# Layer 0's expert stage: the base product cut into 2x2 blocks with seven block products, and two table builds moved behind the first gathers

## The chip, the cores and the metric

The kernel runs on one core of one Trainium2 chip, in one launch. The metric is the device time of that core in microseconds. Most executions of one kernel agree within 0.3%.

## The reference

The input x has 8 sequences of 128 tokens with 512 features, so 1024 tokens. Four layers follow each other, each with a conditioning block whose output goes into an expert block, and the expert block's output is added to x. All data are 32-bit floats. What matters here is the expert block of layer 0 and what stands around it:

```
y    = L0_cond(x)                        # gated feed-forward with low-rank terms, 1376 wide
base = einsum('bsd,od->bso', y, base_W)  # 512 -> 512, the product that is changed
mid  = einsum('bsd,edr->bser', y, lora_A) * top2_weights(softmax(y @ router_W.T))
x    = x + base + einsum('bser,erd->bsd', mid, lora_B) * 2
x    = x + L1_ffn(L1_cond(x))            # low ranks only: needs all of the new x
x    = x + L2_ffn(L2_cond(x, caches))    # attention over a paged cache and the new tokens
x    = x + L3_ffn(L3_cond(x))
```

The attention of layer 2 rotates queries and keys by tables of sines and cosines, and hides cache positions beyond each sequence's length by a mask.

## The kernel before

Activations lie transposed: features on the 128 partitions in four chunks, tokens along the row. `x` is a tile of [128, 4, 1024], and so is `y0`, the output of layer 0's conditioning block. Engine names as in the profile: PE is the matrix engine, DVE the vector engine, ACT the scalar engine, POOL the general engine, which also issues the gathers, and SP issues most transfers.

Many products here are already made in 2x2 blocks with seven block products in place of eight (the Strassen-Winograd scheme): the gate and up products (`gates_by_seven`), the down product (class `Down`), the query, key and value projections and the output projection (`seven`). There each operand is cut into four blocks a11..a22 and b11..b22, four sums s1..s4 of the weight blocks and four differences t1..t4 of the token blocks are made by DVE or POOL, and the seven products are a11b11, s2t2, s1t1, s3t3, a12b21, s4b22 and a22t4. PE accumulates in PSUM; DVE reads half-finished sums out (`u`, `p1`) while PE goes on adding onto the same place.

Layer 0's expert block is made by the helper `experts`, for two halves of 512 tokens, g = 0 and 1. `mids(g)` makes expert ranks and router logits, `route(g)` the top-2 weights on DVE, `mix(g)` turns the weighted ranks so that they can be multiplied again, and `outs(g, os)` makes the output rows: for each of four 128-row chunks `o` a PSUM bank of 512 tokens takes four plain base matmuls and one with `wB` (the experts' second factor). `add_to_x` then adds the bank to `x` on DVE (L305). The order of calls is written out by hand:

```
        mix0(0, large_bank)
        outs0(0, (0, 1), large_bank)
        mids0(1, small_bank)
        route0(1)
        outs0(0, (2, 3), large_bank)
        mix0(1, small_bank)
        outs0(1, (0, 1), large_bank)
        adapted = adapt(0)
        outs0(1, (2, 3), large_bank)
        mids1(0, small_bank)
        route1(0)
        att.begin()
        att.begun(adapted)
```

`adapt(g)` (tile `t1_g`, masked into `l1`) and `mids1`, `route1`, `mix1`, `outs1` are layer 1, which needs the final x of its half. `att.begin` starts the first loads and gathers of attention: the weights, `gather(0, "k")` and `gather(0, "v")` (16 indirect transfers on POOL), and the sums of the projection's weights (`W[0].factors()`, tile `q_s`, L886, on DVE). `att.begun` turns the gathered keys (`kt`, L1119), writes them out and fetches them (`kT`), and issues the next gather, whose buffers are free when `kt` is made.

Ahead of all that, where `attention` is entered, DVE makes the key positions and the mask (`kpos` L820, `hide` L822 and L828) and POOL makes the rotation tables `tsk`, `txk`, `tsq`, `txq` (eight instructions, L838). Their memory is free when layer 0's down product has ended.

A scheduler may move instructions of an engine against each other within what the data allow; those that pass through `kept` or `held` (`tc.keep_in_program_order`) stay in the order of the text.

Of the kernel before, what the change touches and what calls it, by code (L numbers as in the profile page):

```python
# [10 lines left out]
F32 = mybir.dt.float32  # L11
I32 = mybir.dt.int32
AF = mybir.ActivationFunctionType
ALU = mybir.AluOpType
# [3 lines left out]
P = 128  # L18
NB = 8
NT = NB * P  # L20
# [5 lines left out]
HQ, HK, HD = 32, 8, 128  # L26
# [6 lines left out]
NEG = -1e30  # L33
# [14 lines left out]
def forward(ctx: ExitStack, tc: tile.TileContext, a: dict, out: bass.AP):  # L48
    nc = tc.nc
    pe, act, dve, pool, sp = nc.tensor, nc.scalar, nc.vector, nc.gpsimd, nc.sync  # L50
# [13 lines left out]
    wop = ctx.enter_context(tc.tile_pool(name="wop", bufs=1))  # L64
    rp = c1.enter_context(tc.tile_pool(name="rp", bufs=1, side="right"))

    x = xpool.tile([P, DC, NT], F32, tag="x", name="x")
# [4 lines left out]
    st = cg.enter_context(tc.tile_pool(name="st", bufs=2))  # L72
# [34 lines left out]
    for k in range(7):  # L107
        n = 1 << k
# [17 lines left out]
    part = of_partition("part", p_div32, 32.0, ALU.mult, p_mod32)  # L126
# [44 lines left out]
    lens = ints("seqlens", NB)  # L171
# [145 lines left out]
    wmr0 = load_small(ew, "wmr0", [P, DC, 136], chunks(a["wmr0"]), tag="wmr")  # L317
# [5 lines left out]
    with c0:  # L323
# [310 lines left out]
        def psp_bank(shape, name):  # L634
            return psp.tile(shape, F32, tag="mm", name=name)

        HB_ = []
        downs = [Down(0, k) for k in range(2)]

# [20 lines left out]
        downs = [Down(1, k) for k in range(2)]  # L660
        downs[0].begin()
        downs[0].go_on()
        mids0, route0, mix0, outs0 = experts("l0", wmr0, "probs", 2.0, None, wB0, base0, y0, add_to_x)[:4]
        mids0(0, psp_bank)
        route0(0)
        downs[1].begin()
# [9 lines left out]
    with psa:  # L676
# [9 lines left out]


        att = attention(tc, a, x, ident, lens, kvrow, part, ww, wop, ypool, sums, rot, eps, ps_, c2, chunks, mm)

        l1 = att.scratch([P, DC * P + NT], "l1")  # L690
        wa1 = l1[:, 0 : DC * P].rearrange("p (c r) -> p c r", c=DC)
        sp.dma_start(wa1, chunks(a["wa1"]))
# [11 lines left out]
            mid_of=lambda tok: [(t1[:, tok], w11)],  # L704
        )[:4]

        mix0(0, large_bank)
        outs0(0, (0, 1), large_bank)
        mids0(1, small_bank)
        route0(1)  # L710
        outs0(0, (2, 3), large_bank)
        mix0(1, small_bank)
        outs0(1, (0, 1), large_bank)
        adapted = adapt(0)
        outs0(1, (2, 3), large_bank)
        mids1(0, small_bank)
        route1(0)
        att.begin()
# [82 lines left out]
def attention(tc, a, x, ident, lens, kvrow, part, ww, wop, ypool, sums, rot, eps, psa, c2, chunks, mm):  # L801
# [14 lines left out]


    kpos = ap.tile([P, 4], F32, tag="kpos", name="kpos")
    for c in range(4):
        dve.tensor_scalar(kpos[:, c : c + 1], part, float(c * P), None, ALU.add)  # L820
    hide = ap.tile([P, NB, 4], F32, tag="hide", name="hide")
    dve.tensor_tensor(  # L822
        hide,
        kpos.unsqueeze(1).to_broadcast([P, NB, 4]),
        lens.unsqueeze(2).to_broadcast([P, NB, 4]),
        ALU.is_ge,
    )
    dve.tensor_scalar(hide, hide, NEG, None, ALU.mult)  # L828


    tabs = {}
    for m in ("k", "q"):
        ws = ap.tile([P, NB, HD], F32, tag="ts" + m, name="ts" + m)
        wx = ap.tile([P, NB, HD], F32, tag="tx" + m, name="tx" + m)
        for dst, w, tr in ((ws, straight[m], "cos"), (wx, crossed[m], "sin")):
            for i in range(2):
                h = slice(i * 64, (i + 1) * 64)
                pool.tensor_tensor(  # L838
                    dst[:, :, h], w[:, h].unsqueeze(1).to_broadcast([P, NB, 64]), trig[tr], ALU.mult
                )  # L840
        tabs[m] = (ws, wx)


    half = ap.tile([P, 2, REP + 1], F32, tag="half", name="half")
# [23 lines left out]
    def kept(i):  # L868
        return tc.keep_in_program_order(i) if running or i.ins.engine == pool.engine else i
# [38 lines left out]
    def every(ops):  # L908
        for _ in ops:
            pass  # L910

    def gather(n, what):
        qd, p = steps[n]
        t = []
        for j in range(2):
            if what == "k":
                d = kvp.tile([P, 4, HD], F32, tag="kn", name=f"kn_{n}_{j}")
            else:
                d = vals[n % 2 * 2 + j]
            for c in range(4):  # L920
                i = (2 * p + j) * 4 + c
                kept(pool.indirect_dma_start(  # L922
                    out=d[:, c, :], out_offset=None, in_=kc if what == "k" else vc,
                    in_offset=bass.IndirectOffsetOnAxis(ap=kvrow[what][:, qd, i : i + 1], axis=0),
                ))
            t.append(d)
        S[n][what + "c"] = t
# [186 lines left out]
    def turn_cached(n):  # L1114

        s = S[n]
        t = wk.tile([P, 4, 8, 32], F32, tag="kt", name=f"kt_{n}", bufs=1)
        for j in range(2):
            kept(dve.transpose(  # L1119
                t[:, :, 4 * j : 4 * j + 4, :], s["kc"][j].rearrange("p c (b d) -> p b c d", b=4)  # L1120
            ))
        s["kT"] = wk.tile([P, 4, 8, 32], F32, tag="kT", name=f"kT_{n}")
        written(turned[n], t)
        return lambda: kept(sp.dma_start(s["kT"], turned[n].rearrange("b i a m d -> (b i) a m d")))
# [150 lines left out]

    Y = []

    def scratch(shape, name):
        return wk.tile(shape, F32, tag="pT", name=name)

    late = []

    def begin():
        weights(0)
        out_weights(0)
        gather(0, "k")
        gather(0, "v")
        every(W[0].factors())

    def begun(behind):  # L1290

        with tc.issue_after(behind.ins):
            turn_cached(0)()
        gather(1, "k")

    def first(mixed, outs_):
# [1037 lines left out]
```

## Time and profile before

| | |
|---|---|
| three runs | 1492.9, 1496.06, 1497.18 us (median 1496.06) |
| profiled execution | 1490.35 us, its span 1488.6 us |
| granted PE clock | 0.999 |
| PE busy | 1476.6 us, 99% of the span |
| DVE busy | 1065.6 us, 72% |
| POOL busy | 856.4 us, 58% |
| ACT busy | 562.0 us, 38% |
| 243 to 296 us of the span | PE 52.46 us busy of 53, DVE 25.92, POOL 34.53, ACT 4.66 |

Times inside the span count from its first instruction. The stage that is changed lies between 243 and 296 us. In the trace each 32-bit matmul of the program shows as two records, so a row with x8 is four matmuls. A row gives the start, the time until the end of its last record (ends of matmuls are modelled and overlap the next start), the engine, the line, the tiles and the number of records; idle time just ahead of it, and what ended it, stand in square brackets.

### The profile page before, as it was taken

What the parts mean: (1) busy time and instruction counts of PE and PEld (TensorE: products, weight loads), DVE (VectorE), ACT (ScalarE), POOL (GpSimd) and SP (SyncE); (2) the same over time, 40 slices, a digit from 0 to 9 for tenths busy, and PEclk for the clock granted to TensorE, in tenths of its full rate; (3) what the DMA queues carried; (4) which work ended last, traced back from release to release, by engine and by line L of the source; (5) the groups of instructions that cost most, each with busy time, mean ns of one, the idle gap of its engine ahead of it and who ended that gap; (6) DMA issues with size and microseconds to landing.
All of it is one profiled execution on the core that took longest, in us unless ns stands there. A gap on an engine that the chain in (4) does not pass through costs nothing.

```text
span 1488.6 us, 18093 instructions
## 1 busy us (share of the span) xinstructions
PE 1476.6 (99%) x5603; PEld 938.3 (63%) x5603; DVE 1065.6 (72%) x2121; ACT 562.0 (38%) x1422; POOL 856.4 (58%) x876
## 2 busy tenths in 40 slices
PE   9999999999999999999999999999999999999998
PEld 7888787455555655555555555565555555558887
DVE  4665425388888787787778778787878878855475
ACT  1111101044545544454554454454445455431110
POOL 2241104567777777776777777677777777622310
PEclk9999999999999999999999999999999999999999
DMA  7411001213545444564454455345445534433001
GB/s 242 118 44 32 1 1 55 94 36 115 183 148 173 150 119 129 150 183 126 135 152 131 128 158 177 110 135 163 129 125 166 168 106 138 120 104 98 1 9 52
DMA packets 155257, 171.44 MB, mean 115 GB/s; under 512 B 52624, under 2 KB 125776, under 8 KB 155024
## 3 DMA queue, kind: packets, MB, share of 16 engines
q1 hardware_dynamic: 136976, 133.18, 30.0%
q0 software_dynamic: 17056, 36.49, 7.7%
q8 instruction: 47, 0.77, 0.2%
q10 hardware_dynamic: 1120, 0.52, 0.1%
q14 instruction: 58, 0.48, 0.1%
HBM read 129.36 MB, written 40.76 MB: 114 GB/s over the span
## 4 chain that ended last, share of the span: by engine, by line
PE 96%; DVE 2%; ACT 0%; DMA 0%; issue 0%; DVEq 0%; ACTq 0%; SPq 0%
PE st L1173 18%; PE av L1225 18%; PE g L367 9%; PE q_six L979 8%; PE wo_two L979 6%; PE q_one L979 6%; PE q_five L979 6%; PE dn L367 5%; PE wo_six L979 4%; PE wo_one L979 4%; PE eo_l L53 3%; PE z L1761 2%; PE h L1761 2%; PE midp_l L53 1%; PE o L1761 1%; PE gu L367 1%
## 5 line engine op out<-in xcount | busy, mean ns | idle before, releaser
L922 POOL DMA_INDIRECT kn<-in_k_cache,kvrow_k x256 | 272.2, 1063 | 77.1 <-issue 71.2
L922 POOL DMA_INDIRECT vals<-in_v_cache,kvrow_v x256 | 272.3, 1064 | 73.6 <-issue 60.2
L1225 PE MATMUL av<-pT,vals 128*128 128x512 f32 x640 | 290.8, 592 | 0.2 <-DVE oT L1235 0.2
L1177 ACT ACTIVATE pT<-st,hide 128x512 f32<-128x512 f32 x256 | 175.9, 687 | 192.0 <-PE st L1173 178.8
L1173 PE MATMUL st<-qT,kT 128*128 128x512 f32 x512 | 237.4, 596 | 0.0
L1225 PEld LDWEIGHTS av<-pT,vals 128*128 128x128 f32 x640 | 121.4, 190 | 152.7 <-issue 148.3
L1078 POOL TENSOR_TENSOR vq<-q,txq 128x256 f32<-128x256 f32 x128 | 121.1, 976 | 130.6 <-ACT sqq L1052 92.9
L1173 PEld LDWEIGHTS st<-qT,kT 128*128 128x128 f32 x512 | 97.2, 191 | 109.3 <-issue 103.3
L1193 DVE TENSOR_TENSOR part<-pT 128x512 f32<-128x512 f32 x128 | 88.3, 691 | 76.2 <-ACT pT L1177 62.8
L979 PE MATMUL q_one<-q,x 128*128 128x384 f32 x256 | 93.0, 486 | 0.0
L1052 ACT ACTIVATE sqq<-q 128x128 f32<-128x128 f32 x252 | 78.2, 310 | 10.4 <-DVE q L1028 3.8
L979 PEld LDWEIGHTS q_one<-q,x 128*128 128x128 f32 x256 | 48.5, 190 | 39.8 <-issue 14.3
L979 PE MATMUL q_six<-q_s,xs_all 128*128 128x384 f32 x192 | 69.8, 486 | 0.0
L1033 ACT COPY q<-q_one 128x256 f32<-128x256 f32 x32 | 11.9, 372 | 151.9 <-PE q_one L979 133.5
L979 PE MATMUL wo_one<-o,oT 128*128 128x256 f32 x256 | 65.9, 380 | 1.1 <-ACT k L1033 0.8
L1173 PE MATMUL st<-qT,kTn 128*128 128x512 f32 x128 | 65.4, 592 | 0.0
L979 PE MATMUL wo_two<-o_s,os 128*128 128x256 f32 x256 | 60.6, 379 | 0.3 <-DVE os L938 0.3
L1177 ACT ACTIVATE pT<-st,rs 128x512 f32<-128x512 f32 x64 | 44.0, 687 | 38.5 <-PE av L1225 18.5
L979 PEld LDWEIGHTS wo_one<-o,oT 128*128 128x128 f32 x256 | 48.5, 190 | 15.0 <-issue 1.9
L436 POOL TENSOR_TENSOR ws<-wu 128x256 f32<-128x256 f32 (+1 forms) x9 | 6.4, 711 | 86.8 <-DMA wu<-in_WuT 79.8
L1209 ACT COPY rows<-rows 32x32 f32<-32x32 f32 x96 | 20.7, 216 | 92.1 <-DVE rows L1204 91.4
L367 PE MATMUL g<-xs,ws 128*128 128x256 f32 (+1 forms) x240 | 55.1, 379 | 0.0
(461 smaller groups left out, 2838.5 us busy)
## 6 DMA issues: line engine op xcount, KB each, us to landing
turned_new<-qkt SPq DMA_DIRECT2D x120, 160.0 KB
turned_cached<-kt SPq DMA_DIRECT2D x128, 128.0 KB
kT<-turned_cached SPq DMA_DIRECT2D x32, 512.0 KB
R<-sums SPq DMA_DIRECT2D x32, 512.0 KB
qT<-turned_new SPq DMA_DIRECT2D x30, 512.0 KB
q<-in_WqT SPq DMA_DIRECT2D x8, 1024.0 KB
o<-in_WoT SPq DMA_DIRECT2D x8, 1024.0 KB
kn<-in_k_cache,kvrow_k POOLq DMA_INDIRECT x256
```

The costliest lines, as they stand in the source:

```text
L53: pe.matmul(o, lhsT, rhs, start=start, stop=stop)
L367: pe.matmul(o, lhsT, rhs, start=start, stop=stop, skip_group_check=True)
L922: kept(pool.indirect_dma_start(out=d[:, c, :], out_offset=None, in_=kc if what == "k" else vc, in_offset=bass.IndirectOffsetOnAxis(ap=kvro ...
L979: kept(pe.matmul(o, l[:, c, :], r[:, c, :], start=start and c == 0, stop=c == 1, skip_group_check=True))
L1052: kept(act.activation(sq, S[n][m][:, j, i, :], AF.Square, accum_out=S[n]["ssq"][:, j, col : col + 1]))
L1078: kept(pool.tensor_tensor(to, t[:, b, :, hi : hi + 64], wx[:, b, lo : lo + 64].unsqueeze(2).to_broadcast(list(to.shape)), ALU.mult,))
L1173: kept(pe.matmul(ps, s["kT"][:, c, 4 * j : 4 * j + 4, :] if c < 4 else s["kn"][:, j], s["qT"][:, :, REP * j : REP * (j + 1), :].rearrange( ...
L1177: kept(act.activation(pT[:, c, :, :].rearrange("p i t -> p (i t)"), ps, AF.Exp, **(dict(bias=hide[:, b, c : c + 1]) if c < 4 else dict(bia ...
L1193: kept(dve.tensor_tensor(o, l, r, ALU.add))
L1209: kept(act.copy(rows[0:32, g, :], rows[32 * g : 32 * g + 32, 0, :]))
L1225: kept(pe.matmul(ps, v[:, c, :], pT[:, c, :, :].rearrange("p i t -> p (i t)"), start=c == 0, stop=c == NC - 1, skip_group_check=True,))
L1761: return pe.matmul(o, lhsT, rhs, start=start, stop=stop, skip_group_check=True)
```

## The change

Layer 0's base product is made in 2x2 blocks too. `experts` is called without `base` for layer 0, so that its `outs` is no longer used there. `base_sums` makes s1..s4 of the base weights (eight DVE instructions of 256 elements) before `mids0(0)`. `block_sums(g, t)` makes t1..t4 of y0 for a half (four DVE instructions of 512 elements). The class `Based(g, k)` stands for two output chunks of one half: two PSUM banks, `even` and `odd`, each with two halves of 256 tokens. `begin` multiplies a11b11 and copies it to `p1` on ACT. `go_on` makes the other six products, with three DVE reads of half-finished sums between. `finish` adds the `wB` products, lets DVE add `u` or `p1` to x three times from SBUF, and then adds the four PSUM halves to x.

`kpos` and `hide` move into `hidden()`, called from `att.begun`; the rotation tables move into `tabled()`, called at the end of `att.begin`, behind the first 16 gathers; `W[0].factors()` moves from `att.begin` to the end of the block in `att.begun`.

```
+        A0 = base_sums()
-        mids0, route0, mix0, outs0 = experts("l0", ..., wB0, base0, y0, add_to_x)[:4]
+        mids0, route0, mix0, _, _, T0 = experts("l0", ..., wB0, None, y0, None)
...
+            def into(self, o, l, r, start=False):
+                for c in range(2):
+                    pe.matmul(o, l[:, c, :], r[:, c, :], start=start and c == 0, stop=False, skip_group_check=True)
+
+            def begin(self):
+                self.into(self.even[:, 0], A0[self.k][0], self.b[0][0], True)
+                held(act.copy(self.p1, self.even[:, 0]))
+                return self
+
+            def go_on(self):
...
+                self.into(odd[:, 1], s1, t1, True)
+                self.into(odd[:, 0], s2, t2)
+                held(dve.tensor_tensor(u, odd[:, 0], p1, ALU.add))
+                held(dve.tensor_tensor(p1, odd[:, 1], p1, ALU.add))
+                self.into(even[:, 1], s3, t3)
+                held(dve.tensor_tensor(p1, even[:, 1], p1, ALU.add))
+                self.into(odd[:, 1], s4, b22)
+                self.into(even[:, 0], a12, b21)
+                self.into(even[:, 1], a22, t4)
+
+            def finish(self):
...
+                    pe.matmul(ps, wB0[...], T0[g][...], start=False, stop=True, skip_group_check=True)
+                for t, _, more in at.values():
+                    if more is not None:
+                        held(dve.tensor_tensor(t, t, more, ALU.add))
+                for t, ps, _ in at.values():
+                    held(dve.tensor_tensor(t, ps, t, ALU.add))
...
+        based = [Based(0, k).begin() for k in range(2)]
+        block_sums(0, [yt0[:, n] for n in range(4)])
         mix0(0, large_bank)
-        outs0(0, (0, 1), large_bank)
         mids0(1, small_bank)
+        for b in based:
+            b.go_on()
+            b.finish()
         route0(1)
-        outs0(0, (2, 3), large_bank)
+        block_sums(1, [t[:, n] for t in yt1 for n in range(2)])
+        based = [Based(1, k).begin() for k in range(2)]
         mix0(1, small_bank)
-        outs0(1, (0, 1), large_bank)
+        based[0].go_on()
+        based[0].finish()
         adapted = adapt(0)
-        outs0(1, (2, 3), large_bank)
+        based[1].go_on()
+        based[1].finish()
         mids1(0, small_bank)
...
     def begin():
         weights(0)
         out_weights(0)
         gather(0, "k")
         gather(0, "v")
-        every(W[0].factors())
+        tabled()

     def begun(behind):
         with tc.issue_after(behind.ins):
             turn_cached(0)()
+            hidden()
+            every(W[0].factors())
         gather(1, "k")
```

As built, PE has nineteen rows more, the scheduler puts a product of the next block into some of the gaps (two of block (0,1) ahead of s4b22 of block (0,0)), POOL's eight table instructions stand behind the first 16 gathers and ahead of the next eight, and SP's load of the first output weights (`o`), which waits for the last base matmul, stands ahead of the last of the four writes of `kt`. From the turn of layer 1's first half (`mix1(0)`) on, every engine's order is the same as before.

## The prediction

> **What bounds the kernel now.** The page's busy times and its chain that ended last come first.
>
> ```profile
> PE 1476.6 (99%) x5603; PEld 938.3 (63%) x5603; DVE 1065.6 (72%) x2121; ACT 562.0 (38%) x1422; POOL 856.4 (58%) x876
> PE 96%; DVE 2%; ACT 0%; DMA 0%; issue 0%; DVEq 0%; ACTq 0%; SPq 0%
> ```
>
> PE is the bound: idle 12.0 us of 1488.6, and 96% of the chain. So work taken from PE counts in full, work put on DVE, ACT or POOL counts only where PE then waits for it, and time won elsewhere counts for nothing. Next the stage itself, in the timelines of PE and of DVE and POOL.
>
> ```profile
> 212.14 2.32 PE L367 MATMUL dn<-h,wds 128*128 128x256 f32 x10
> 214.30 2.32 PE L367 MATMUL dn<-h,wd 128*128 128x256 f32 x10
> ...
> 255.80 3.60 PE L53 MATMUL eo_l<-y,base 128*128 128x512 f32 x8
> 259.23 1.02 PE L53 MATMUL eo_l<-midT_l,wB 128*128 128x512 f32 x2
> 260.09 3.60 PE L53 MATMUL eo_l<-y,base 128*128 128x512 f32 x8
> ...
> 291.19 0.73 PE L53 MATMUL midp_l<-w,l 128*128 128x136 f32 x4 [0.47 <-DVE l L309]
> ```
> ```profile
> 210.25 0.42 DVE L609 TENSOR_TENSOR du_dn<-dn,dp_dn 128x256 f32<-128x256 f32 x1 [5.23 <-PE dn L367]
> 210.71 0.42 DVE L610 TENSOR_TENSOR dp_dn<-dn,dp_dn 128x256 f32<-128x256 f32 x1
> ...
> 244.91 0.95 DVE L822 TENSOR_TENSOR hide<-kpos,seqlens 128x32 f32<-128x32 f32 x1
> 245.89 1.17 DVE L828 TENSOR_SCALAR hide<-hide 128x32 f32<-128x32 f32 x1
> 251.42 3.25 DVE L886 TENSOR_TENSOR q_s<-q 128x768 f32<-128x768 f32 x2 [2.73 <-DMA q<-in_WvT]
> 254.60 1.94 DVE L886 TENSOR_TENSOR q_s<-q,q_s 128x768 f32<-128x768 f32 x2
> ```
> ```profile
> 250.65 3.21 POOL L838 TENSOR_TENSOR txq<-wx_q,sin 128x512 f32<-128x512 f32 x2
> 279.09 0.94 POOL L922 DMA_INDIRECT kn<-in_k_cache,kvrow_k  x1 [4.10 <-DVE kt L1119]
> ```
>
> PE's groups stand start to start without a gap: eight records of 512 columns take 259.23 - 255.80 = 3.43 us (0.429 each), ten of 256 take 2.16 us (0.216 each). Half the columns cost half the time; the smaller matmul pays 1 ns. The only wait of PE that the timeline shows between 243 and 296 us is 0.47 us. DVE is busy 25.92 of these 53 us.
>
> **PE's work.** Removed are eight groups of base products (four chunks, two halves), 8 x 3.43 = 27.4 us. Added are four blocks of seven products of two matmuls, 4 x 7 x 2 x 2 = 112 records of 256 columns, 112 x 0.2158 = 24.2 us. The `wB` products go from 16 records of 512 (6.87 us) to 32 of 256 (6.91 us). On PE: **-3.25 us**. All of it is on the path.
>
> **Sums of the base weights.** Eight DVE instructions of 0.42 us, 3.4 us. Their tile takes over the place of the down product's weight sums, whose last reader for chunk pair 0 ends near 214.3 us. DVE then has nothing until the logits at 224.67 (idle 11.90 us there). They lie under PE's `dn` groups: nothing; without that cover, 3.4 us.
>
> **Differences of y0.** Half 0: four DVE instructions of 512 elements, 0.69 us each, behind the last copy of y0 at 244.55, so until 247.3. Meanwhile PE has two a11b11 (1.73 us), the turn of the ranks (0.43) and `midp` (3.7), from 243.0 to 248.9: nothing. Half 1's four stand 5 us and more ahead of their use: nothing.
>
> **The hand-overs.** In each block PE must wait, before s4b22, until DVE has read both halves of `odd`, and before a22t4 until it has read s3t3. I lay PE's built order against DVE's, with 0.34 us start to start for independent 256-element instructions and 0.46 where one needs the one before (both in the rows of `y<-dn` and `du_dn`, `dp_dn`). Block (0,0): PE has s3t3 and one product of block (0,1) in between, 1.73 us; DVE needs 0.04 to see the end, two reads and one instruction of `route0(1)` between them, about 1.9: PE waits 0.2. Block (0,1): cover 2.2 us, but two differences of half 1 (0.6 to 0.69 each) stand between the reads: 0.1. Block (1,0): cover s3t3 and a quarter of `adapt(0)`, 1.73 us against 0.9: nothing. Block (1,1): cover 1.3 us; the mask of `l` and two `kt` (1.9 us) stand ahead of the reads, and they are just in time: nothing, with 0.1 us to spare. Sum **+0.3 us**.
>
> **The tail of the stage.** `q_s` moves from 251 us, where DVE had time, to about 280 to 286, four instructions of 0.95. They stand among the last block's adds and ahead of layer 1's first `route`. That chain ends in `mw_l`, which PE needs for its next turn of ranks. It ends about 288 us in the new time, while PE's last `t` ends 0.6 us earlier. PE's small waits here were about 0.8 us in all (0.47 shown, the rest under 0.2 each) and become 1.1: **+0.3 us**. From the other side: the same line has taken 943 to 2017 ns. At 2.0 us four of them bring 4.3 us more, of which PE would wait for all; at the low end nothing. I take 0.95, since the long ones stand beside POOL's arithmetic and POOL issues gathers here.
>
> **The moved tables and mask.** The 16 gathers begin 10.7 us earlier (POOL's tables took 243.31 to 253.80); nobody waited for them, as `kt` at 278.12 follows `t` of PE: gain nothing. The eight table instructions now run from about 263 to 274 us, ahead of `gather(1, "k")`, which waits for `kt` (about 278) anyway; they are used at 304 us: nothing. The mask is used at 320 us: nothing. On SP the load of `o` now holds one write of `kt` back until the last base matmul, about 282 us; the fetch of `kT` goes out at about 286, as now (285.35), and its use is at 316 us: nothing.
>
> What can cost is the neighbourhood of tables and DVE. In the rows above `hide` takes 0.95 and 1.17 us for 32 elements while the tables run, where such a size takes 0.19 elsewhere (`e_l`), and two `q_s` take 3.25 us against 1.94 for the next two; the adds from PSUM in the same stretch (`y<-dn`, 0.42) are not slower. [...] I take 0; the upper end, if a read stands behind a delayed add, is 2 us.
>
> **Sum.** -3.25 + 0.3 + 0.3 = -2.65 us, 0.18% of the profiled execution (1490.35; span 1488.6). Behind the stage PE has no gap before the end and keeps the gain. The three runs had a median of 1496.06, 5.7 above the profiled one; on that median I predict **1493.4 us**. Differences within 0.3% (4.5 us) are about what a measurement of this kernel can tell from no change, so the likeliest true effect is a gain that lies inside that band.
>
> **Rivals.** (1) The saving is given back: the hand-overs and the tail cost as much as PE gains, with `q_s` at its median 1.46 us (4 x 0.5 = 2 us) and 1 us more of waits: 1496.1. For it: the cover is one or two products of 0.86 us, where the down product, made in the same way without a PE wait, had 2.16 us for each. Against: the order laid out above leaves only tenths. (2) Slower: DVE becomes the bound of the stage. DVE's work rises by the blocks' 4 x 10 x 0.42 = 16.8 us, the differences' 5.5, less eight adds of 0.69, from 25.9 to 42.7 us in about 50. If DVE runs late at every hand-over by one blocked instruction (1.23 us, the table's), eight hand-overs cost 9.8 us: -3.25 + 9.8 gives +6.6, 1502.6. It decides from 0.97 us of mean delay on, (4.5 + 3.25) / 8. Against: only two hand-overs lie within the table's 11 us, and DVE still has 7 us of idle time. (3) The change does not save PE time, because twice as many, smaller matmuls pay a fixed price: the 0.429 and 0.216 us speak against it; at 10 ns a record the 64 records more cost 0.6 us, so this cannot turn the sign.
>
> More than -3.25 - 0.8 = -4.1 us can't come, since PE's waits in the stage are no more than 0.8 us.
>
> **How the numbers follow.** The forecast has 0.73, rival 1 0.16, rival 2 0.11, rival 3 is inside the forecast. Under the forecast the true effect lies inside the band, but the three runs lie from 3.2 below to 1.1 above their median, and the edge (1491.6) is only 1.8 us below my number: I give 0.31 to a measured gain over 0.3%, 0.41 to the band and 0.01 to a loss. Rival 1 gives 0.03, 0.11 and 0.02; rival 2 0.01 to the band and 0.10 to a loss. Together 0.34 faster, 0.53 the same, 0.13 slower. The range goes from 1489.0 (the largest gain, 1492.0, less 3 us of spread) to 1499.0 (rival 1 with 3 us more for the long `q_s`); rival 2 is left out.
>
> **What would show it.** PE busy falls by 3.2 us; rows of `b_..` at 0.216 us a record; in the stretch from the end of `dn` to the first `q_one` PE idle about 1.4 us, in brackets behind DVE; base sums between 214 and 222 us; tables near 263 to 274 with DVE's adds slowed beside them; the first `st` 2.7 us earlier than 318.90. Wrong would be: waits of 1 us or more at s4b22 or a22t4 (rival 2), `q_s` of 1.5 us or more with a PE wait behind `mw_l` (rival 1), records of 256 columns above 0.22 us (rival 3), or a difference that arises behind 320 us, where I expect none.

## The result, and the profile after

The changed kernel takes 1512.80 us (median of 6 runs, 1508.42 to 1516.68) against 1494.52 us for the kernel before: ratio 1.0115, 95% interval 1.0099 to 1.0130. It is slower by 1.15%, and the medians lie 18.3 us apart, where a gain of 2.65 us was forecast. The profiled execution took 1514.16 us with a span of 1512.4 us, 23.8 more than the profiled execution before (1488.6).

First the page of the changed kernel: busy times, and the chain that ended last.

```profile
PE 1480.8 (98%) x5667; PEld 954.0 (63%) x5667; DVE 1087.0 (72%) x2169; ACT 563.5 (37%) x1426; POOL 855.4 (57%) x876
PE 91%; DVE 4%; DMA 2%; issue 1%; another core or an unknown queue 1%; SPq 0%; ACT 0%; POOL 0%; DVEq 0%; ACTq 0%
```

PE's busy time has not fallen by 3.2 us but risen by 4.2, though it does less arithmetic, and its share of the chain went from 96 to 91%, DVE's from 2 to 4. Where that happens shows in the timeline of PE (start, time, records, and in brackets the idle time before and what ended it).

```profile
249.78 3.62 PE L728 MATMUL b<-yt,base0s 128*128 128x256 f32 x16
258.93 2.08 PE L728 MATMUL b<-y,base0s 128*128 128x256 f32 x4 [5.53 <-DVE b0u L742]
263.93 2.07 PE L728 MATMUL b<-y,base 128*128 128x256 f32 x4 [2.93 <-issue]
...
280.68 2.08 PE L728 MATMUL b<-y,base0s 128*128 128x256 f32 x4 [7.49 <-DVE b0u L743]
```

Three waits of 15.95 us in all: before s4b22 and a22t4 of block (0,0), and before s4b22 of block (0,1). They cost more than their length: sixteen records ahead take 3.6 us, 0.22 each, but four records behind a wait take 1.86 us start to start (263.93 to 265.79), 0.47 each. The windows (PE, PEld, DVE, ACT, POOL busy, then the granted clock) show why.

```profile
258.00:263.00 5.00, 2.08 (x4) 1.18 (x4) 1.20 (x4) 0.00 (x0) 3.78 (x5) 0.58 0.16 53
263.00:268.00 5.00, 4.07 (x10) 3.27 (x11) 4.55 (x4) 0.00 (x0) 4.68 (x5) 0.50 0.12 37
...
278.00:283.00 5.00, 2.32 (x6) 1.87 (x7) 4.66 (x13) 0.00 (x0) 0.00 (x0) 0.50 0.02 5
```

The granted clock is 0.58, 0.50 and 0.50 in these three windows (1.00 in 253 to 258 us), so PE is "busy" for longer with the same work. Now the other side of the hand-over, DVE and ACT, and POOL beside them.

```profile
253.99 0.42 DVE L266 TENSOR_TENSOR r_l<-r_l,lower 128x256 f32<-128x256 f32 x1
257.78 0.42 DVE L742 TENSOR_TENSOR b0u<-b,b0u 128x256 f32<-128x256 f32 x1 [3.37 <-remote]
...
263.45 0.42 DVE L745 TENSOR_TENSOR b0u<-b,b0u 128x256 f32<-128x256 f32 x1 [4.25 <-remote]
...
263.91 11.33 DVE L765 TENSOR_TENSOR x<-x,b0u 128x256 f32<-128x256 f32 x3
```
```profile
252.06 0.39 ACT L241 COPY mid_l<-midp_l 128x272 f32<-128x272 f32 x1 [3.31 <-PE b L728]
```
```profile
263.83 0.96 POOL L1020 DMA_INDIRECT vals<-in_v_cache,kvrow_v  x1 [0.30 <-issue]
264.80 2.50 POOL L937 TENSOR_TENSOR tsk<-ws_k,cos 128x512 f32<-128x512 f32 x2
...
272.15 2.47 POOL L937 TENSOR_TENSOR txq<-wx_q,sin 128x512 f32<-128x512 f32 x2
```

Two different things went wrong. The addition at L742 waits for nothing but PE's s2t2, which is the second quarter of the sixteen records at 249.78 and over by about 251.5; yet DVE begins at 257.78, 6 us later, and the profile finds no releaser ("remote"). ACT's copy of `midp`, whose records end at about 249.9, begins 2.1 us late in the same way. And the three additions at L765, which take 1.1 us together when alone, take 11.33 us here. One of them alone is held for 10.7 us: nearly the whole stretch of the eight table instructions (264.80 to 274.62).

From the start of the last `dn` record to the start of the first `q_one`, "the stage" from here on, the profile before has 242.71 to 295.65, 52.9 us; the profile after has 243.50 to 316.17, 72.7 us. Of the 23.8 us more, 19.7 arise here, 0.8 before and 3.3 behind.

### The profile page after: what moved, and what is told of

The parts are those of the page before. It is cut to its first block, busy times and chain, and to the rows that moved or that the text cites. A ratio compares the mean times of both kernels' runs of the same rounds, so it can differ in the third digit from the quotient of the medians.

```text
span 1512.4 us, 18286 instructions
## 1 busy us (share of the span) xinstructions
PE 1480.8 (98%) x5667; PEld 954.0 (63%) x5667; DVE 1087.0 (72%) x2169; ACT 563.5 (37%) x1426; POOL 855.4 (57%) x876
## 4 chain that ended last, share of the span: by engine, by line
PE 91%; DVE 4%; DMA 2%; issue 1%; another core or an unknown queue 1%; SPq 0%; ACT 0%; POOL 0%; DVEq 0%; ACTq 0%
PE st L1271 17%; PE av L1323 17%; PE g L367 9%; PE q_six L1077 8%; PE q_one L1077 5%; PE q_five L1077 5%; PE wo_two L1077 5%; PE dn L367 5%; PE wo_one L1077 3%; PE wo_six L1077 3%; PE h L1861 2%; PE z L1861 2%; PE o L1861 1%; PE midp_l L53 1%; PE b L728 1%
## 5 line engine op out<-in xcount | busy, mean ns | idle before, releaser
L1020 POOL DMA_INDIRECT vals<-in_v_cache,kvrow_v x256 | 272.4, 1064 | 73.6 <-issue 59.3
```

Source lines behind the costliest of these rows:

```text
L1020: kept(pool.indirect_dma_start(out=d[:, c, :], out_offset=None, in_=kc if what == "k" else vc, in_offset=bass.IndirectOffsetOnAxis(ap=kvro ...
```

## The experiments

Kernels that were sent together (a set) ran on the same chip beside the kernel before. In some of these sets what waited for PE began at once (within 0.1 us of the record's end, on time below), in others 2 to 9 us late in parts of the stage (late below) in every kernel whose gathers run beside the blocks; so times are compared within a set, and each run below says which of the two its set was. The kernel before took 1489.09 and 1489.38 us in the sets on time and 1491.21 to 1494.52 us in the late ones and in the result. Theory 1 is that the tables hold DVE instructions beside them (one addition for 10.7 us in the profile after), a cost that the prediction had put at nothing; the rivals are the early gathers (theory 2, later 4) and hand-overs that are too tight in themselves (theory 3).

### First set: blocks alone, moves alone, two other places for the tables

**e1**, everything moved is put back:

```diff
+    hidden()
+    tabled()
...
     def begin():
-        tabled()
+        every(W[0].factors())
     def begun(behind):
-            hidden()
-            every(W[0].factors())
```

> The blocks as changed, but mask, rotation tables and the sums q_s where they stood before (tables ahead of the first gathers). Theory 1 (lock): adds of two SBUF tiles on DVE are held while POOL's tables stand back to back beside the blocks. Theory 2 (early gathers): gathers that begin 10 us earlier delay DVE's reads (waits of 3.4 and 4.3 us with no releaser). Theory 3 (blocks): the hand-overs themselves are too tight. Before is about 1494.5. By 1 and 2 no long add and no waits at the hand-overs, 1491 to 1493; by 3 waits of several us at s4b22 stay, 1500 or more.

Measured: 1494.64 us, ratio 1.0034 (1.0022 to 1.0046), stage 57.6 us, on time. DVE, then POOL, then PE:

```profile
246.24 1.82 DVE L772 TENSOR_TENSOR yt<-y 128x512 f32<-128x512 f32 x1
248.09 1.65 DVE L772 TENSOR_TENSOR yt<-y,yt 128x512 f32<-128x512 f32 x1
```
```profile
245.01 2.50 POOL L937 TENSOR_TENSOR txk<-wx_k,sin 128x512 f32<-128x512 f32 x2
247.46 3.41 POOL L937 TENSOR_TENSOR tsq<-ws_q,cos 128x512 f32<-128x512 f32 x2
```
```profile
257.71 2.08 PE L728 MATMUL b<-y,base0s 128*128 128x256 f32 x4 [3.32 <-DVE b0u L743]
```

Beside the tables a difference of y0 takes 1.65 to 1.82 us for 0.69, and two table instructions take 3.41 for 2.5. From 246.24 to 253.01 us DVE makes four differences, 1.57 to 1.85 us start to start, and POOL's last four table instructions take 6.75 us: in these rows the two engines take turns, one instruction each. The first hand-over is 3.3 us late, and the four records behind it take 2.08 us, where four take 1.13 in e3. The blocks alone, with the old places, lose 5.6 us against the kernel before (1489.09).

**e2**, the plain base product with the moves; the edit is against the kernel before:

```diff
... (the bodies of mask and tables become hidden() and tabled())
         gather(0, "k")
         gather(0, "v")
-        every(W[0].factors())
+        tabled()
...
             turn_cached(0)()
+            hidden()
+            every(W[0].factors())
         gather(1, "k")
```

> The plain base product as before, but mask, tables and q_s moved as in the change. Theory 1: nothing of two SBUF tiles that PE waits for lies beside the tables, so within 1 us of before (1493.5 to 1496). Theory 2: the ACT copy and DVE steps of the second half's route come 2 to 8 us late, but PE has base matmuls in front of it: 0 to +4 us. Theory 3: the same as before.

Measured: 1489.59 us, ratio 1.0004 (0.9992 to 1.0016), stage 52.8 us, on time. The moves alone cost nothing that these runs can tell.

**e3**, the tables by memsets in the same place:

```diff
-                    kept(pool.tensor_tensor(dst[:, :, h], ..., trig[tr], ALU.mult))   # eight
+            for dst in tabs[m]:
+                kept(pool.memset(dst, 0.5))                                           # four
```

> As changed, but the rotation tables are not computed: four POOL memsets stand in their place (the rotation is left out, and POOL reads no SBUF there). Theory 1: the 10.7 us add falls to 0.42 us and PE's wait of 7.5 us with its half clock goes: about 1501 to 1503, the waits of 3.4 and 4.3 us stay. Theory 2 alone: the long add is part of the same delay and stays in some form, 1508 or more. Theory 3: as changed, about 1512.

Measured: 1485.29 us (one run), stage 50.1 us, on time. PE, then DVE:

```profile
248.04 3.62 PE L728 MATMUL b<-yt,base0s 128*128 128x256 f32 x16
251.64 1.13 PE L728 MATMUL b<-y,base0s 128*128 128x256 f32 x4
```
```profile
250.16 0.42 DVE L266 TENSOR_TENSOR r_l<-r_l,lower 128x256 f32<-128x256 f32 x1
250.50 0.42 DVE L742 TENSOR_TENSOR b0u<-b,b0u 128x256 f32<-128x256 f32 x1
```

This is the stage that the prediction had laid out: no wait at a hand-over, 2.9 us shorter than before.

**e4**, POOL waits for u of the first block, then tables, then gathers:

```diff
     def begin(after):
+        kept(pool.tensor_scalar(ap.tile([P, 10], ...), after[:, 0:10], 1.0, 0.0, ALU.mult, ALU.add))
+        tabled()
         gather(0, "k")
         gather(0, "v")
-        tabled()
```

> As changed, but POOL first waits for the first block's read (a small POOL instruction that reads u), then makes the tables, and only then issues the first gathers: tables beside the blocks, no gathers there. Theory 1: an add of x and u is held about 8 to 10 us, the waits without releaser go: about 1500 to 1506. Theory 2: no delay at all, 1491 to 1494. Theory 3: as changed, about 1512.

Measured: 1495.66 us (one run), stage 59.3 us, on time. DVE's three additions take 4.36 us and what follows is late in turn, so block (0,1) pays (the view ends behind the first two of these four records):

```profile
253.53 4.36 DVE L765 TENSOR_TENSOR x<-x,b0u 128x256 f32<-128x256 f32 x3
```
```profile
267.04 1.22 PE L728 MATMUL b<-y,base0s 128*128 128x256 f32 x2 [6.81 <-DVE b0u L743]
```

After this set theory 1 looked sufficient: the gathers stood as early in e3 as in the changed kernel and cost nothing.

### Second set: the tables out of the way

**e5** is the changed kernel, unedited.

> The changed kernel itself, on the chip of this call. In its first profile two VectorE instructions of the hand-over waited 3.4 and 4.3 us for something the profile couldn't name, before the tables began; only thereby did the adds of u and p1 to x of the first block fall beside the tables (10.7 us held). Theory 1 (the tables alone): those two waits belong to the kernel's own order and come back, PE waits 5 to 7 us at the s4 records again, about 1510 us. Theory 2 (the early gathers beside the loads of the attention weights disturb VectorE and ScalarE): the same time, and the two waits are seen again before the tables. Theory 3 (the two waits belonged to that execution or that chip): without them the tables begin behind the adds of both first blocks and meet only the three adds of the third, about 1487 to 1492 us.

Measured: 1509.40 us, ratio 1.0102 (1.0074 to 1.0130), stage 69.7 us, late. The two "remote" waits are there again (2.6 and 2.8 us); theory 3 of that expectation falls. The instruction that the tables hold is now another one, the next DVE instruction with two inputs in SBUF:

```profile
264.17 10.56 DVE L772 TENSOR_TENSOR yt_r<-y,yt_r 128x512 f32<-128x512 f32 x1
```

**e6**, `tabled()` behind `gather(1, "k")`.

> The changed kernel with the eight table instructions put behind the gathers of the second step's keys, some 24 us later on GpSimd (about 288 to 299 us of the span), behind all eight hand-overs of the blocks. Theory 1 (the tables exclude VectorE's instructions with two inputs in SBUF, and its hand-overs come late): no PE wait over 1 us at the s4 records, the stage as with the memsets; what the tables meet now is the four sums xs and mw_l of layer 1, about 1 us each, most of it under PE's expert records: 1485.5 to 1489 us. Theory 2 (the gathers that start at 243 us beside the loads disturb VectorE): the late hand-overs stay, over 1495 us.

Measured: 1508.21 us, ratio 1.0103 (1.0081 to 1.0126), stage 59.9 us, late. Theory 2's number, and theory 1 at work elsewhere: the tables (298.07 to 307.9) hold the first sum for the attention weights, and PE waits 6.5 us in the attention product.

```profile
301.15 7.02 DVE L1036 TENSOR_TENSOR xs<-x 128x256 f32<-128x256 f32 x1
```
```profile
310.34 2.93 PE L1077 MATMUL q_six<-q_s,xs 128*128 128x384 f32 x4 [6.48 <-DVE xs L1036]
```

**e7**, the tables on DVE, two at each of four points where it waited for PE in e3:

```diff
-                    kept(pool.tensor_tensor(
+                    tc.keep_in_program_order(dve.tensor_tensor(
...  (in finish(), blocks (0,1) and (1,0))
+                if g + k == 1:
+                    list(itertools.islice(tables, 2))      # behind the adds of u and p1, and again behind the copies
```

> The changed kernel with the eight table instructions on VectorE instead of GpSimd, two behind each of four points of the second and third block, where VectorE waited 1.8 to 2.6 us for PE in the run with memsets; 0.69 us each by the rows of 128x512 there, 1.3 us for two. Theory 1: GpSimd computes nothing in the stage, so nothing excludes VectorE; no PE wait over 1 us, the forecast's gain in full: 1485 to 1487 us. Theory 2 (early gathers): over 1495 us, as the gathers stand where they stood. Theory 3 (the hand-overs themselves are too tight for VectorE): 5 us more VectorE work in the stage shows as PE waits at a22 t4 or wB, 1488 to 1493 us.

Measured: 1500.20 us, ratio 1.0049 (1.0030 to 1.0069), stage 59.9 us, late. The third wait is gone, the first two are not:

```profile
258.27 1.76 PE L728 MATMUL b<-y,base0s 128*128 128x256 f32 x4 [4.77 <-DVE r_l L267]
261.85 2.08 PE L728 MATMUL b<-y,base 128*128 128x256 f32 x4 [1.82 <-issue]
```

So without any table on POOL 6.5 us of loss remain (1500.20 - 1493.73, the kernel before in this set). Theory 1 is not enough.

**e8**, e1 with `every(W[0].factors())` left behind in `begun`.

> The blocks with tables and key mask in their old place and only the four sums q_s of the attention weights moved behind. It splits the loss of the run with everything in the old place (ratio 1.0034): there the tables met the four yt (1.75 us each for 0.69) and then two q_s stood between the hand-overs. Theory 1 (exclusion by the tables carries it): yt again 1.65 to 1.8 us each, PE waits of 0.5 to 0.6 us twice before s1 t1, most of the loss stays: 1490 to 1493 us. The rival, that the q_s between the hand-overs carry it: the wait of 3.3 us at s4 b22 goes and the time falls to 1486 to 1488 us.

Measured: 1505.54 us, ratio 1.0080 (1.0058 to 1.0103), stage 62.4 us, late. The `yt` rows are those of e1 (1.82 us and so on) and the wait of 3.3 us at the first s4b22 stays, so the `q_s` were not its cause. But a new wait of 5.2 us stands at s4b22 of block (1,0), behind a DVE addition with 4.3 us of "remote", around the last of the gathers, which run from 255.9 to 276.5 us in this kernel. PE, then DVE:

```profile
258.39 1.13 PE L728 MATMUL b<-y,base0s 128*128 128x256 f32 x4 [3.31 <-DVE b0u L743]
279.88 2.07 PE L728 MATMUL b<-y,base0s 128*128 128x256 f32 x4 [5.24 <-DVE b0u L743]
```
```profile
278.94 0.43 DVE L742 TENSOR_TENSOR b0u<-b,b0u 128x256 f32<-128x256 f32 x1 [4.34 <-remote]
```

The delay went with the gathers to another block. The gathers stand in their old place here, so it is not their move alone that costs: against e1, on time, the stage is 4.8 us longer.

### Third set: gathers fewer, and gathers none

**e9** is the changed kernel, unedited.

> The changed kernel unedited, as the mark for the three other kernels on this call's chip. In its two profiles so far VectorE's u addition began 5.3 us or more behind the end of the PE records that it waits for, and ScalarE's copy of the router's product 2.1 us behind, while GpSimd issued its gathers; in the run with memsets, on another chip, both began at once. Theory 4 (the gathers hold back the signals by which PE tells the others that a record has ended): the delays are there again, about 1508 us. Theory 5 (a property of the chip, whatever GpSimd does): if this chip is one without them, 1485 to 1495 us, with the tables meeting only a few additions.

Measured: 1505.76 us, ratio 1.0086 (1.0065 to 1.0106), stage 67.4 us, late: on the chip of the first set, so the chip does not decide, and theory 5 falls.

**e10**, e7 with `gather(0, "v")` behind `gather(1, "k")`.

> The changed kernel with the tables on VectorE, as in the run before at ratio 1.0049, and the eight gathers of the values behind the second keys' gathers; only the eight gathers of the first keys run in the stage, to about 254 us instead of 264. Theory 4: PE's signals are late only up to about 254 us; the wait at s4 b22 of the first block falls from 4.8 to about 1 to 2 us, the one at a22 t4 goes, no half clock: 1486 to 1490 us. Theory 5: the waits of the run before (4.8 and 1.8 us) return unchanged, 1498 to 1500 us, or none are there in either kernel.

Measured: 1499.54 us, ratio 1.0044 (1.0029 to 1.0060), stage 56.9 us, late. POOL's last gather of this run, then DVE:

```profile
252.68 0.96 POOL L1027 DMA_INDIRECT kn<-in_k_cache,kvrow_k  x1 [0.30 <-issue]
```
```profile
255.21 0.42 DVE L742 TENSOR_TENSOR b0u<-b,b0u 128x256 f32<-128x256 f32 x1 [1.92 <-remote]
256.54 0.41 DVE L745 TENSOR_TENSOR b0u<-b,b0u 128x256 f32<-128x256 f32 x1
```

L742 comes 1.6 us after the last gather and everything after it at once; the wait at a22t4 is gone. The one at s4b22 shrank only to 3.9 us, and the four records behind it took 2.07 us; the time did not meet theory 4's 1486 to 1490 us. PE also waits 2.0 us in the attention product, beside the second run of gathers.

**e11**, e7 with ordinary loads of the same bytes by SP's queue for the first sixteen gathers:

```diff
+                if n == 0:
+                    kept(sp.dma_start(d[:, c, :], (kc if what == "k" else vc)[i * P : (i + 1) * P, :]))
+                    continue
                 kept(pool.indirect_dma_start(
```

> The changed kernel with the tables on VectorE and the sixteen gathers of the first step replaced by sixteen ordinary loads of as many bytes by SyncE's queue; it leaves out the look-up of the cache rows in the first step. Theory 4 with the gathers of GpSimd as the cause: no delay of PE's signals, no PE wait over 1 us between 243 and 290 us, about 1485 to 1488 us. If the bytes and not the gathers are the cause: the waits stay as with gathers, 1496 to 1500 us.

Measured: 1496.88 us (one run), stage 50.0 us: not one wait over 0.4 us in it, in a set whose other three kernels were late. PE, then DVE:

```profile
252.06 3.62 PE L728 MATMUL b<-yt,base0s 128*128 128x256 f32 x16
255.66 1.13 PE L728 MATMUL b<-y,base0s 128*128 128x256 f32 x4
```
```profile
254.52 0.42 DVE L742 TENSOR_TENSOR b0u<-b,b0u 128x256 f32<-128x256 f32 x1
```

Theory 4 holds for the stage, by one execution here and by e15. The loads move the same bytes beside the first hand-over (249 to 259 us) and delay nothing. The single time is 5.05 us over the kernel before's median (1491.83), but not by the stage: 3 us were lost ahead of it (last `dn` at 245.8, in e9, e10 and e12 at 242.3 to 242.7) and some 6 behind it (1199.0 us to the end of the span, 1193.0 in the profile before).

**e12** is e3 again.

> The changed kernel with the four rotation tables written by memsets, so without the rotation, as run once on another chip (1485.29 us, no wait). It joins the two calls. Theory 4 with delays that this chip shows beside gathers: the gathers stand where they stand in the changed kernel, so the waits of 4.8 and about 1.8 us before the s4 and a22 records of the first block return, about 1497 to 1500 us, some 10 us under the changed kernel, and that difference is the tables' exclusion alone. Theory 1 (the tables are all of the loss): no PE wait over 1 us, 1485 to 1488 us on this chip too.

Measured: 1499.42 us, ratio 1.0054 (1.0036 to 1.0073), stage 59.6 us, late. The same kernel had a stage of 50.1 us in the first set.

```profile
255.35 1.13 PE L728 MATMUL b<-y,base0s 128*128 128x256 f32 x4 [3.15 <-DVE b0u L743]
257.52 2.07 PE L728 MATMUL b<-y,base 128*128 128x256 f32 x4 [1.04 <-issue]
269.02 1.13 PE L728 MATMUL b<-y,base0s 128*128 128x256 f32 x4 [3.20 <-DVE b0u L743]
```

Against e9 in the same set, the tables' own part is 67.4 - 59.6 = 7.7 us of stage (67.38 - 59.64).

### Fourth and fifth set: gathers behind the first block

**e13**, e7 with POOL waiting for u of block (0,0) as in e4, then the gathers of the first keys; those of the first values stand behind `roots(0)`. **e14**, the same with the gathers of the values directly behind those of the keys:

```diff
     def begin(after):
+        kept(pool.tensor_scalar(ap.tile([P, 10], ...), after[:, 0:10], 1.0, 0.0, ALU.mult, ALU.add))
         gather(0, "k")
-        gather(0, "v")        # e13: moved behind roots(0); e14: stays
```

> The changed kernel with the tables on VectorE; GpSimd waits for u of the first block before it issues the gathers of the first keys (252 to 262 us of the span), and the gathers of the first values stand behind the roots, at about 309 us. Never more than eight gathers run on end in the stage, none beside the loads of the attention weights and the first block's hand-over. Theory 4 (the gathers hold back PE's signals, more with each that follows): no PE wait over 1 us between 243 and 290 us, from the last down product to the first attention product 50 to 52 us; 1487 to 1490 us, where the values' gathers do not come late for their product at about 325 us. Rival (the blocks' hand-overs are late in any case): a wait of 2 us and more at an s4 or a22 record, a stage of 56 us and more.

> The same, with the gathers of the first values directly behind those of the first keys: sixteen on end, 252 to 272 us. Theory 4: the first block's hand-over is free of waits, but behind the first ten or twelve gathers, from about 266 us on, PE's signals come 2 to 5 us late, and the hand-over of the third block (s4 or a22 at about 268 to 272 us) waits 2 to 5 us, as in the run with early tables and late sums: a stage of 53 to 58 us, 1491 to 1496 us. Rival (only the loads beside the gathers matter): no wait, 50 to 52 us, 1487 to 1490 us.

Measured, on time: e13 1494.23 us, ratio 1.0030 (1.0019 to 1.0041), stage 50.1 us; e14 1486.51 us, ratio 0.9985 (0.9975 to 0.9994), stage 50.0 us. Both stages are free of waits, so they say nothing on late signals. e13's late gathers push POOL's rotation of the second step back, and PE waits there:

```profile
333.09 2.37 PE L1259 MATMUL turned<-ident,r 128*128 128x128 f32 x10 [4.31 <-DVE r L1218]
```

**e15** is e11 again, timed.

> The kernel with ordinary loads for the first step's gathers once more (it leaves out the look-up of cache rows in the first step), now timed beside the others. Its one look had no wait of PE in the stage, 50.0 us of it, and yet 1496.88 us, with a span that lost 3 us ahead of the stage and some 6 us in the attention steps, where nothing was edited. Theory 4: the stage is 50 to 51 us again and the time comes to 2 to 4 us under the kernel before. Rival (the later load of the keys costs the attention steps): over 1493 us again.

Measured: 1488.61 us, ratio 0.9996 (0.9987 to 1.0006), stage 50.0 us, on time. The stage is as expected, the time only 0.8 us under the kernel before's: the gain is lost outside the stage. Against e14 in the same set 1.5 us are lost ahead of it (last `dn` at 243.5 against 242.0) and 3.1 behind it (1194.0 us to the end of the span against 1190.9). Why was not followed up.

**e16** is e2 again.

> The kernel with the plain base product and the moved tables, mask and gathers, which measured a ratio of 1.0004 in the first call, where no profile had late signals. Theory 4 with theory 1: the plain product hands nothing over inside a product, so late signals and held additions of VectorE cost PE less than 2 us even where this call's gathers delay them: ratio 1.000 to 1.002. Rival (the moves cost by themselves where the gathers delay): ratio 1.004 and more, PE waits for free accumulators of over 3 us between 243 and 290 us.

Measured: 1489.11 us, ratio 0.9998 (0.9989 to 1.0007), stage 52.8 us, on time, and all of PE's waits from 235 to 330 us are one line:

```profile
PE midp_l L53 <- DVE l L309: 0.3, 1, 0.3
```

The last set had the changed kernel (**e17**) beside e14 again (**e18**), to catch both under the same signals.

> The changed kernel unedited, as the mark for this call. All its profiles so far had PE's signals late (2 to 9 us) while gathers ran; the kernels of the first and the fourth call had none late, gathers or not. If they are late here: 1504 to 1512 us as before. If they are on time here: the first blocks hand over at once as in the run with memsets, the tables (264 to 274 us) meet only the three additions of the third block and the copies behind them; these come up to 7 us late, and PE waits for the accumulators of the third block at the last one's wB or a22: a stage of 50 to 57 us for 53 before, 1486 to 1494 us.

> The kernel with the tables on VectorE and the sixteen gathers behind the first block's hand-over, which took 1486.51 us at a ratio of 0.9985 where signals were on time. If they are on time again: the same, 0.998 to 0.9995. If this call's are late: theory 4 (late behind ten or more gathers on end) has the third block's hand-over wait 2 to 5 us, a stage of 53 to 58 us, a ratio of 1.000 to 1.004; if only the loads beside the gathers make them late, no wait, a stage of 50 to 51 us and a ratio of 0.998 to 0.9995.

Measured, both late: e17 1508.75 us, ratio 1.0106 (1.0083 to 1.0128), stage 69.7 us; e18 1501.54 us, ratio 1.0066 (1.0049 to 1.0083), stage 59.8 us. The views of e18: PE, DVE, and POOL's last gather.

```profile
268.49 1.02 PE L53 MATMUL t<-x,l 128*128 128x512 f32 x2
277.33 2.08 PE L728 MATMUL b<-y,base0s 128*128 128x256 f32 x4 [7.81 <-DVE b0u L743]
```
```profile
267.04 1.28 DVE L944 TENSOR_TENSOR txk<-wx_k,sin 128x512 f32<-128x512 f32 x2
276.39 0.42 DVE L742 TENSOR_TENSOR b0u<-b,b0u 128x256 f32<-128x256 f32 x1 [8.06 <-remote]
```
```profile
273.19 0.94 POOL L1028 DMA_INDIRECT vals<-in_v_cache,kvrow_v  x1 [0.30 <-issue]
```

The two blocks that hand over before the ninth gather do so at once; behind it DVE stands still for 8.1 us, until 2.3 us after the last gather (273.19 + 0.94). PE's records do not stand still: those of `t` start at 268.49 without a gap, behind the hand-over that L742 waits for. What comes late is the signal. The trace records PE's semaphore updates there at 264.91, 266.35, 267.78, 269.92, 276.30 and 276.35 us, which, measured from PE's own records, is 0.6, 1.1, 2.1, 3.8, 8.5 and 7.7 us later than the same updates in e14; and DVE and ACT begin 0.02 to 0.09 us behind these updates. That is theory 4's place (the third block), no loads beside it; the size was expected at 2 to 5 us. So e14's gain was seen only where signals were on time, and no version that was measured in both kinds of set beats the kernel before in both.

The stage in all profiles (us from the last `dn` to the first `q_one`). The profile before stands under late by its trace: on-time traces hold some 22,000 semaphore updates, late ones 10,800 to 11,700, and that of the kernel before 11,127.

| POOL in the stage | on time | late |
|---|---|---|
| plain product, old order (before) or moves (e2, e16) | 52.8, 52.8 | 52.9 (before) |
| blocks, no tables, no gathers by POOL (e11, e15) | 50.0 | 50.0 |
| blocks, gathers of keys alone, no tables on POOL (e13; e10) | 50.1 | 56.9 |
| blocks, all sixteen gathers, no table arithmetic on POOL in the stage (e3, e14; e6, e7, e12, e18) | 50.1, 50.0 | 59.9, 59.9, 59.6, 59.8 |
| blocks, gathers, tables on POOL (e1, e4; e8; changed kernel four times) | 57.6, 59.3 | 62.4; 67.4 to 72.7 |

## Why the prediction was wrong, point by point

**PE's work: right.** 0.216 us a record at full clock, and where nothing interferes the stage is 52.9 - 50.0 = 2.9 us shorter, for 2.65 forecast. The hand-overs (0.3 us) and the tail (0.3 us) of the sum came out smaller still: in e3 and e14 PE's only wait is 0.4 us ahead of the turn of ranks, where the kernel before waits 0.47. But e3 leaves the tables out and e14 makes them on DVE; the changed kernel itself was never seen so.

**Base sums, differences of y0, mask, late q_s: right**, in the places that they have in the changed kernel.

**"I take 0" for the tables: the first step that failed.** They were priced at nothing, at most 2 us, and no run shows a term of that size; they cost 7.7 us of stage (e9 against e12) and 9.8 (e5 against e7, 69.7 - 59.9), both in late sets. Two things were missed. One is how long a single DVE instruction can be held beside the tables. In e1 the rows go turn by turn, 1.65 to 1.82 us for 0.69. In the changed kernel they do not: one instruction was held 10.7 us beside all eight, back to back (10.6 in e5, 5.9 in e9). And behind the held instruction, in DVE's order, stand the next block's L742 and L743 (in the profile after, the four additions of the PSUM halves to x too), for which PE waits at s4b22: 7.5 to 7.8 us in all four profiles. The prediction's 2 us were an estimate for a read behind a delayed addition, far below that.

**The gathers at "gain nothing": the second step, and the larger one.** The prediction moved sixteen gathers 10.7 us ahead, beside the first hand-over, and asked only who waits for their data. In three sets of five, and in the profile after, what waits for PE comes late while they run: 59.8 - 50.0 = 9.8 us of stage with no table on POOL. e11 against e10 in one set, and the moved place in e8 and e18, tie it to the gathers; e11 is one execution. The profile before had no sign of it. Its trace is of the late kind too, its gathers run from 254 to 275 us, and yet the readers of PE's sums begin at once there, PE, DVE and POOL:

```profile
263.52 1.02 PE L53 MATMUL eo_l<-midT_l,wB 128*128 128x512 f32 x2
264.58 0.69 DVE L305 TENSOR_TENSOR x<-eo_l,x 128x512 f32<-128x512 f32 x1 [2.28 <-issue]
264.07 0.95 POOL L922 DMA_INDIRECT kn<-in_k_cache,kvrow_k  x1 [0.30 <-issue]
```

Only DVE's masking of `t` into `l` is late, by 0.5 us (277.51), just behind the last gather. So gathers beside late signals are not the whole condition: they did this beside the blocks and not beside the plain product, and why is open.

**"Behind the stage PE has no gap": not quite.** The changed kernel loses 3.3 us there. Each profile of a kernel with blocks, seventeen in all, has one wait of 1.4 us ahead of a `midp_l` late in the span (at 1384 us in e14) that those of the kernel before, e2 and e16 do not have. In the fourth set e14 is 2.8 us shorter than e16 in the stage and 1.65 longer behind it (1190.9 against 1189.25 us to the end of the span). The cause of that wait was not looked for.

**A cost that was in no term: the half clock.** e18's stage is 9.8 us longer than e14's for 7.8 us of waiting; e17's is 19.6 longer for 14.6. So a long wait costs 2.0 to 2.5 us more. The mean granted clock from 243 to 320 us is 1.00 in e14, 0.96 in e18 and 0.91 in e17. Waits of 3.15 and 3.20 us in e12 and of 3.31 in e8 left the next four records at full clock (1.13 us for the four), and those of 3.32 us in e1 and 7.81 in e18 did not (2.08). But a short wait soon after a long one brought half clock too, 1.04 us in e12 (2.07 us for the four) and 1.75 in e9:

```profile
255.10 1.13 PE L728 MATMUL b<-y,base0s 128*128 128x256 f32 x4 [2.47 <-DVE r_l L267]
257.98 2.07 PE L728 MATMUL b<-y,base 128*128 128x256 f32 x4 [1.75 <-issue]
```

The length of one wait alone does not set the clock here, and what does is not shown.

**Rival 2 was the right kind, at 0.11.** It named DVE late at the hand-overs by table instructions, for 9.8 us spread over eight. Its 1.23 us for each is the author's estimate, one table instruction (two take 2.47 us in the profile after); no run shows a delay of that size at every hand-over. In the changed kernel it came as three waits of 1.5 to 7.8 us; only the last (7.5 to 7.8) is the tables', and the first two are the late signals, which it did not name. What was held against it, two hand-overs beside the tables and 7 us of idle DVE, is an argument from averages: one stall in DVE's order moves everything behind it.

Not settled: why PE's signals come late beside the gathers in some sets and not in others, and whether the recording of the trace, which holds half as many updates there, has a part in it; and what the changed kernel takes with signals on time, which none of its four profiles caught. By e1 and e4 it would still lose where the tables meet DVE.

## What to carry to other kernels

A product that hands partial sums to another engine and waits for them inside itself has bought arithmetic with slack: before cutting it so, count how many microseconds of independent records stand between each hand-over and its return, and ask what a delay of 5 us there costs, the half clock behind it included (2.0 to 2.5 us a wait here). When work of POOL is moved, price its neighbours and not only its readers: list the DVE instructions beside it (those held for 5.9 to 10.7 us here had two inputs in SBUF) and all that stands behind them in DVE's order. And a gain of 0.2% that rests on tenths of slack is to be measured in several sets: e3, e12, e14 and e18 are two kernels that won in one set and lost in the other.

## What the runs showed of the hardware

- One DVE instruction with two SBUF inputs was held beside eight (10.7 us in the profile after, 10.6 in e5) or the last five to six (7.0 us, e6) POOL table instructions in a row; in e1, e4 and e8 the same two forms took turns (1.65 to 1.82 us for 0.69 on DVE, 2.7 to 3.4 for 2.5 on POOL). What decides between the two is not known.
- In late sets DVE and ACT began 2 to 9 us behind the end of the PE records that they wait for while POOL issued gathers beside the blocks, and at once again 1.6 to 2.8 us after the last gather (e10, e18, e9, e12). In e18 the first eight gathers delayed nothing, and PE's semaphore updates were recorded as late as the readers began. Plain loads of the same bytes by SP delayed nothing (e11).
- Behind a long wait of PE the next 256-column records took 0.43 to 0.47 us instead of 0.216: in the stage behind every wait from 3.32 us up (in e7 and e17 for some of the four records only), not behind the waits of 2.47 to 3.31 us that stood alone, but behind 0.8 to 2.0 us too where a longer wait stood shortly before.
